# Four hybrid layers on one core: shared weight preparation, a merged second layer and a shorter buffer ring

## The chip, the cores and the metric

The kernel runs on one core of one Trainium2 chip, as a single launch. The metric is the device time in microseconds (us) of that launch. A profile of one execution gives the span from the first to the last instruction and, for each engine, what it did and what it waited for. The engines are PE (matrix products, with weight loads counted apart), DVE (vector), ACT (activations), POOL (a second vector engine) and SP, which here only issues transfers between DRAM and on-chip memory (SBUF). Products land in PSUM, in banks of 128 x 512 f32.

## The reference

The input is x of shape (4, 96, 64, 64). Four layers follow each other, and each adds its result to the stream. Batches never mix.

```python
# layer 0: layer norm, in_proj to xi and z, depthwise 3x3 conv, silu, selective scan, gate, MLP
xs = rows, columns, and both reversed           # 4 directions, 192 channels, 16 states
hst = hst * dA + dBx;  y_t = einsum('bkdn,bkn->bkd', hst, C_t)     # over 4096 steps
t = t + (layernorm(y_sum) * silu(z)) @ out_proj;  t = t + mlp(layernorm(t))
# layer 1: group norm, then
xc, z = in_proj(x);  u = silu(conv3x3(xc))
h = dA_l * h + dBu_l                            # 2 directions, 96 channels, 1 state
y = layernorm(y_forward + y_backward);  y = y * silu(z);  x = x + out_proj(y)
# layer 2: layer norm, relu(bn(x @ w1)), FFT over the 4096 tokens, complex relu, inverse FFT,
#          @ w2, bn; then layer norm and an MLP with e5m2 operands and f16 results ("ffn")
# layer 3: layer norm, linear attention (no softmax), then the same kind of ffn
```

## The kernel before, in words

**Two streams of work.** The *foreground* is the selective scan of layer 0: 64 steps (4 batches, 4 directions, 4 chunks of 1024 tokens), 24 units each, 1536 units in all. For a unit, `sources` has POOL multiply u and B into a tile `w`; `decays` has ACT form exp(dt A) into `h` in PSUM; `recurs` has DVE run the scan and then multiply by C into `w` (for every twelfth unit POOL does this product, in `side`); `gathers` has PE sum over states into `py`; `collects` adds that into `Y`. `preludes` makes dt, B and C for a step. The `w` tiles are a ring of `WB` = 7: POOL can write a tile again only when PE has read it. After each last-direction chunk, `Y` is stored to `y_d`; for batch 3, chunk 0 it stays in SBUF.

The *background* is everything else, in `others`: `front(b)` (norm, projection and conv of layer 0) for all batches, then `rest(b)` for batch after batch: `tail` (gate and MLP of layer 0, `gate(c)` for four chunks of 1024 and `group(g)` for eight groups of 512 tokens), `l1`, `l2_front`, `l2_middle`, `back`. `tail(b)` waits for the stores of `y_d`.

**The order** on every engine is fixed when the program is made. `Work` holds threads (generators). Each asks for an engine with `yield on(...)`, possibly with events, PSUM banks and a time. `Work.choose` takes the thread whose next piece could start first by estimated durations; ties go to the lower rank. What is then issued stands in order on that engine's queue, and an instruction that has to wait holds up everything behind it. `par(jobs, n, wide)` runs a list of jobs with n threads. While the foreground runs, the background has three PSUM banks (`bm`). When it has ended, five more (`be`) are opened and `mode["wide"]` is set: more threads, and elementwise work of the background goes to DVE instead of POOL (`spare`).

**Weights.** Each `rest(b)` loads its weights and prepares some: `tail` computes an MLP bias and centres `m1` (products with `cent` and a copy), `l1_weights2` multiplies two factors into `dtc`, `l2f_weights` folds a batch norm into `w1` (from a load `bn`, broadcast to 97 rows), `back_weights` folds another into `w2` and makes `wqt`, `wkv` and `vb`. For the last batch all but the tail's are made by `early`, right after the foreground.

**Layer 1 in the foreground's time** has stages with a barrier between: `inproj` (8 groups into the padded image `xp`), `conv` (9 matmuls per group and a silu into `u`), then 16 pieces: 8 forward, whose results stay in SBUF as `yf`, and 8 backward, which also finish the layer: centring, variance, the z projection into PSUM with its silu, the gate (`scalar_tensor_tensor(a, a, ..., pz)`), output projection, store to `t_d`. `l2_front` then loads `t_d` again for a layer norm into `xa` (`ln`), with a barrier, and computes the first FFT stage (`dft`). In wide mode conv already runs beside the pieces, and the pieces do the layer norm.

Lines in the profile are those of helpers: L205 is `mm`, L209 `copy`, L220 `act`, L217 its table load, L232 any DVE or POOL operation, L253 and L257 loads and stores. So work is told apart by tile names: `w<-u,bb` is POOL's product, `h<-h,state,w` a scan, `x_d`, `t_d` the stores of `x1_d` and `t_d`, `a<-a,vec,bm` the gate with z, `sc`, `var`, `vb`, `m`, `bias` the weight preparation.

## Time and profile before

| what | us |
|---|---|
| median of 3 runs | 6828.23 (6811.11 to 6831.17) |
| profiled execution, its own time | 6820.0 |
| its span | 6818.2 |
| DVE busy | 5834.1 (86%) |
| POOL busy | 4989.7 (73%) |
| PE busy | 5155.3 (76%), weight loads 1600.5 |
| ACT busy | 4259.4 (62%) |
| last scan of the foreground starts | 6167.8 |
| mean granted PE clock | 0.844 of full |

Busy times are shares of the whole span[...]. In a row of a group, the numbers behind the bar are the busy time in us, the mean duration of one in ns, and the idle time of that engine just before those instructions with what ended it. The scan's DVE rows carry most of the span. Up to about 140 us there is a start-up; after 6173 only batch 3 is left.

### The profile page before, as it was taken

The numbers are of one execution on the slowest core, as the hardware profiler recorded it, in microseconds if no ns is written. First come the engines' busy times: TensorE is split into PE (matmuls) and PEld (weight loads), VectorE is DVE, ScalarE is ACT, GpSimd is POOL, SyncE is SP. The second block draws the span as 40 slices with busy tenths as digits, with TensorE's granted clock in tenths as the row PEclk, the third lists the DMA queues.
The fourth block names the chain that finished last, engine by engine and source line by source line (L and its number), as shares of the span: only waits on it lengthen the run. The fifth ranks groups of instructions, "written<-read, shape, count | busy, mean of one in ns | idle before, by whom it ended". The sixth has DMA issues, their size and how long they took to land. (4 is left out here: it accounts for less than half of the span.)

```text
span 6818.2 us, 54968 instructions
## 1 busy us (share of the span) xinstructions
PE 5155.3 (76%) x15312; PEld 1600.5 (23%) x15312; DVE 5834.1 (86%) x3961; ACT 4259.4 (62%) x6433; POOL 4989.7 (73%) x2322
## 2 busy tenths in 40 slices
PE   7878897566866878768857787767876687777788
PEld 2222221111211332212201232212211133212263
DVE  3999999999998999999989999999989899992613
ACT  3757565465656557767656566776665555775735
POOL 2788888888897778887898777888789777871000
PEclk8889999687878999779878998877887898878888
DMA  5565555555545685565554586556555477533351
GB/s 161 186 197 180 189 176 178 164 181 172 166 148 156 216 263 159 163 191 177 167 159 148 173 280 193 165 166 194 162 157 155 152 234 248 173 111 82 114 154 34
DMA packets 522211, 1166.82 MB, mean 171 GB/s; under 512 B 90416, under 2 KB 163628, under 8 KB 521904
## 3 DMA queue, kind: packets, MB, share of 16 engines
q1 hardware_dynamic: 521904, 1163.31, 55.3%
q8 instruction: 122, 2.00, 0.1%
q14 instruction: 185, 1.52, 0.1%
HBM read 928.74 MB, written 234.36 MB: 171 GB/s over the span
## 5 line engine op out<-in xcount | busy, mean ns | idle before, releaser
L232 POOL TENSOR_TENSOR w<-u,bb 128x1024 f32<-128x1024 f32 x1536 | 3608.9, 2370 | 829.3 <-PE py L205 742.7
L232 DVE TENSOR_TENSOR_SCAN h<-h,state,w 128x1024 f32<-128x1024 f32 x1056 | 2480.4, 2349 | 149.7 <-ACT h L220 112.6
L205 PE MATMUL py<-w,sel 128*32 128x512 f32 x6144 | 1895.6, 953 | 788.9 <-DVE w L232 542.1
L220 ACT ACTIVATE h<-dt,negA 128x1024 f32<-128x1024 f32 x1536 | 1725.6, 1124 | 439.1 <-DVE w L232 378.2
L232 DVE TENSOR_TENSOR w<-h,cc 128x1024 f32<-128x1024 f32 x1408 | 1722.0, 1223 | 101.5 <-DVE h L232 3.7
L232 DVE TENSOR_TENSOR_SCAN h<-h,w 128x1024 f32<-128x1024 f32 x352 | 805.2, 2288 | 83.3 <-ACT h L220 72.1
L209 ACT COPY state<-h 128x1 f32<-128x1 f32 x1056 | 166.4, 158 | 906.5 <-DVE w L232 902.3
L205 PEld LDWEIGHTS py<-w,sel 128*32 128x32 f32 x6144 | 195.5, 117 | 1977.9 <-DVE w L232 1103.4
L232 POOL TENSOR_TENSOR w<-w,cc 128x1024 f32<-128x1024 f32 x128 | 301.5, 2355 | 105.6 <-ACT state L209 90.8
L205 PE MATMUL bm<-xp,dg 128*128 128x512 f32 x792 | 365.2, 610 | 1.3 <-ACT xi L220 1.3
L205 PE MATMUL bm<-xi,xw 128*128 128x512 f32 x384 | 233.9, 758 | 132.0 <-DMA xi<-xi_d 123.5
L205 PE MATMUL bm<-xd,dtw 64*128 64x512 f32 x384 | 230.2, 689 | 20.7 <-ACT dtu L220 7.2
L232 POOL TENSOR_TENSOR dtu<-dtu 128x1536 f32<-128x1536 f32 x64 | 221.7, 3464 | 30.1 <-ACT dtu L220 18.4
L220 ACT ACTIVATE dtu<-bm 128x512 f32<-128x512 f32 x384 | 208.3, 596 | 48.5 <-PE bm L205 45.2
L232 DVE TENSOR_TENSOR_SCAN w<-h,state,w 128x1024 f32<-128x1024 f32 x96 | 224.8, 2341 | 13.8 <-POOL w L232 7.1
L232 POOL MEMSET y<- 1x4096 f32 x4 | 14.1, 3514 | 291.7 <-DMA g_d<-o 291.6
L232 POOL TENSOR_TENSOR dtu<-dtu,xi 128x1536 f32<-128x1536 f32 x64 | 221.9, 3467 | 0.2
L205 PE MATMUL bm<-x,cent 96*96 96x512 f32 x318 | 183.8, 676 | 48.6 <-POOL x L232 13.7
L205 PE MATMUL bm<-xp,l1dg 96*96 96x512 f32 x468 | 215.8, 607 | 1.2 <-ACT u L220 1.2
L205 PEld LDWEIGHTS bm<-xp,dg 128*128 128x128 f32 x792 | 146.8, 192 | 267.8 <-issue 257.0
L232 POOL TENSOR_TENSOR Y<-Y,yt 128x512 f32<-128x512 f32 x141 | 182.8, 1296 | 29.4 <-ACT yt L209 28.2
L220 ACT ACT_TABLE_LOAD x131 | 168.1, 1283 | 20.3 <-PE bm L205 14.7
(356 smaller groups left out, 6956.2 us busy)
## 6 DMA issues: line engine op xcount, KB each, us to landing
u<-dd SPq DMA_DIRECT2D x384, 512.0 KB
dt<-dd SPq DMA_DIRECT2D x384, 512.0 KB
bb<-bc SPq DMA_DIRECT2D x256, 512.0 KB
cc<-bc SPq DMA_DIRECT2D x256, 512.0 KB
dd<-dtu SPq DMA_DIRECT2D x256, 384.0 KB
xi<-xi_d SPq DMA_DIRECT2D x256, 192.0 KB
f_d<-fo SPq DMA_DIRECT2D x64, 384.0 KB
a<-f_d SPq DMA_DIRECT2D x64, 384.0 KB
```

Of the source, the lines that this page charges most:

```text
L205: return nc.tensor.matmul(o, lhsT=lhsT, rhs=rhs, **kw)
L209: return nc.scalar.copy(o, i, **kw)
L220: return nc.scalar.activation(o, i, func, **kw)
L232: return f(o, *a, **kw)
```

## The change

It prepares the weights of the later layers once (`prepare`, in the background after `front(0)`), keeps them in one DRAM tile `prep` and loads them in packed pieces (`parcel`); constants that used to be loaded one by one are packed on the host. In layer 1, silu(z) is computed in `inproj`, stored to `z1_d` and loaded into a piece's own SBUF tile; forward results go to `y1_d` and come back; conv and pieces run together in both modes; backward pieces also do layer 2's norm. `xp` and `xa` share one tile, `big`. `dft` has three threads instead of two, the two f16 layers four instead of three, and `xq` lies inside `buf`. `WB` goes from 7 to 6. The diff, cut:

```diff
+    def fetch(self, load):
+
+        t = self.me
+        was = t.end, t.start, t.last
+        load()
+        t.start, t.last = was[1:]
...
+    prep = dram.tile([128, PREP], F32, name="prep_d")
+    y1_d = [dram.tile([C, L], F32, name=f"y1_d{b}") for b in range(B)]
+    z1_d = [dram.tile([C, L], F32, name=f"z1_d{b}") for b in range(B)]
...
-    def given(key, weights, wp, temp):
+    def given(key, weights, wp):
...
-        st, (wb,) = pools(bg(temp))
-        got = yield from weights(wp, wb)
-        st.close()
+        return (yield from weights(wp))
...
+    def parcel(wp, name, src, cols, sizes):
+
+        n = sum(w for _, w in sizes)
+        t = wp.tile([128, n], F32, name=name)
+        get(t, src[:, cols : cols + n])
+        got, c = [], 0
+        for rows, w in sizes:
+            got.append(t[0:rows, c : c + w])
+            c += w
         return got
...
     def tail(b, stat):
...
-        get(m1, I["mlp1T"])
-        get(wo, I["wo"])
-        get(m2, I["mlp2T"])
-        (pb,) = yield on("pe", banks=1)
-        for f in range(3):
-            mm(pb[:, f : f + 1], lhsT=m1[:, f * 128 : f * 128 + 128], rhs=V("b2", C), start=True, stop=True)
-        bias = wp.tile([128, 3], F32, name="bias")
-        yield on("dve")
-        ve.tensor_add(bias, pb[:, 0:3], V("mb1", n=3))
-        ve.tensor_scalar(m1, m1, V("g2", C), None, ALU.mult)
-        drop(pb)
-        yield from centred(m1, m1, 384)
+        wo, m2 = parcel(wp, "rt", I["r_tail"], 0, [(128, 6 * C), (128, 3 * C)])
+        m1, bias = parcel(wp, "pt", prep, 0, [(C, 384), (128, 3)])
+        wo = wo.rearrange("p (h j c) -> p h j c", h=2, j=3)
+        m2 = m2.rearrange("p (f c) -> p f c", f=3)
...
-    def l1_weights(wp, wb):
...
+    def l1_weights(wp):
...
-        get(gavg, I["c_gavg"])
-        get(w_in, I["l1_inT"])
-        get(dg, I["l1_dg"])
-        return gavg, w_in, dg
...
-    def l1_weights2(wp, wb):
...
-        yield on("pool")
-        po_.memset(dtc, 0.0)
...
-        (pw,) = yield on("pe", banks=1)
-        for k in range(2):
-            mm(pw[0:C, k * C : (k + 1) * C], lhsT=xr[:, k], rhs=dr[:, k], start=True, stop=True)
-        yield on("act")
-        copy(dtc[0:C, :, 0:C], pw[0:C, 0 : 2 * C].rearrange("p (k c) -> p k c", k=2))
-        drop(pw)
-        return w_out, dtc
...
-    def l1(b, stat, pp):
+        gavg, w_in, w_out = parcel(wp, "rl1", I["r_l1"], 0, [(C, C), (C, DI), (C, C)])
+        (dtc,) = parcel(wp, "pl1", prep, 387, [(C + 1, 2 * (C + 4))])
+        return gavg, w_in, w_out, dtc.rearrange("p (k c) -> p k c", k=2)
...
+    def l1(b, stat, pp, big):
         wide = mode["wide"]
-        stu, (pu,) = pools(bg("l1u"))
-        u = pu.tile([C + 1, L], F32, name="u")
-        st, (wp,) = pools(bg("l1c"))
-        xp = wp.tile([C, 66, 66], F32, name="xp")
-        gavg, w_in, dg = yield from given("l1", l1_weights, (pp, wp), "l1b")
+        u = pp.tile([C + 1, L], F32, name="u")
+        xp = big[0:C, 0 : 66 * 66].rearrange("p (h w) -> p h w", w=66)
+        xa = big[:, 0:L]
+        gavg, w_in, w_out, dtc = yield from given("l1", l1_weights, pp)
         mv = pp.tile([C, 2], F32, name="mv")
         gm = pp.tile([C, 4], F32, name="gm")
         bias = pp.tile([C, 2], F32, name="l1bias")
+        st, (wp, wk) = pools(bg("l1c"), bg("l1w"))
+        dg = wp.tile([C, 9, C], F32, name="dg")
...
+            po_.memset(big[C : C + 1], 1.0)
             po_.memset(u[C : C + 1], 1.0)
...
-        stx, (wk,) = pools(bg("l1cw"))
+        yield on("sp")
+        get(dg, I["l1_dg"])
 
         def inproj(g):
             def job(t):
-                x = wt(wk, C, "x", t)
+                x, z = wt(wk, C, "a", t), wt(wk, C, "dt", t)
+                s = slice(g * HC, (g + 1) * HC)
                 yield on("sp")
-                get(x, x1_d[b][:, g * HC : (g + 1) * HC])
+                get(x, x1_d[b][:, s])
...
+                post("l1x", b, g)
+                (pz,) = yield on("pe", banks=1)
+                mm(pz[0:C], lhsT=w_in[:, C : 2 * C], rhs=x, start=True, stop=True)
+                yield on("act", took=0.7, table=AF.Silu)
+                act(z, pz[0:C], AF.Silu, bias=bias[:, 1:2])
+                drop(pz)
+                yield on("sp")
+                put(z1_d[b][:, s], z)
 
...
-        yield from par([inproj(g) for g in range(NG)], 4, 8)
-        stx.close()
...
                 s = slice(q * HC, (q + 1) * HC)
+                near = ("l1x", b, min(q + 1, NG - 1))
                 if wide and t == 0:
+                    yield on("dve", near)
                     yield from taps(u[0:C, s], xp, 8 * q, V("l1cw", C, n=9))
-                    yield on("act", table=AF.Silu)
...
-                    return
-                (pc,) = yield on("pe", banks=1)
...
+                    pc = u[0:C, s]
+                else:
+                    (bank,) = yield on("pe", near, banks=1)
+                    pc = bank[0:C]
...
+                act(u[0:C, s], pc, AF.Silu, bias=V("l1cb", C))
+                if not (wide and t == 0):
+                    drop(bank)
                 post("l1u", b, q)
...
-        convs = par([conv(q) for q in range(NG)], 2)
-        if wide:
-            wk_.add(convs)
-        else:
-            yield from convs
-            st.close()
-
-        st2, (wp, wk) = pools(bg("l1s"), bg("l1sw"))
-        yf = wp.tile([C, L], F32, name="yf")
-        w_out, dtc = yield from given("l1s", l1_weights2, wp, "l1sb")
-        if wide:
-            xa = ahead["l2f"][4]
+        yield from par([inproj(g) for g in range(NG)], 3, 8)
+        convs = wk_.add(par([conv(q) for q in range(NG)], 2))
...
+                e2, name = spare()
                 yield on(name)
+                e2.tensor_mul(dt, a, cc[0:C])
                 if k == 0:
-                    e2.tensor_mul(yf[:, s], a, cc[0:C])
-                    post("l1y", b, g)
+                    yield on("sp")
+                    put(y1_d[b][:, s], dt)
+                    post("l1y", b, g, stored=True)
                     return
-                e2.tensor_mul(dt, a, cc[0:C])
-                x = bb
-                yield on("sp")
+                x, yf = bb, cc[0:C]
+                yield on("sp", ("l1y", b, g))
+                get(yf, y1_d[b][:, s])
                 get(x, x1_d[b][:, s])
-                pc, pv = yield on("pe", ("l1y", b, g), banks=2)
+                pc, pv = yield on("pe", banks=2)
                 mm(pc[0:C], lhsT=cent, rhs=dt, start=True, stop=False)
-                mm(pc[0:C], lhsT=cent, rhs=yf[:, s], start=False, stop=False)
+                mm(pc[0:C], lhsT=cent, rhs=yf, start=False, stop=False)
...
                 mm(pv[0:C], lhsT=avg, rhs=a, start=True, stop=True)
+                wk_.fetch(lambda: get(yf, z1_d[b][:, s]))
                 yield on("act", took=1.4, table=LN_EXP)
                 rstd(a, pv[0:C])
                 drop(pv)
                 yield on("dve")
                 ve.scalar_tensor_tensor(a, pc[0:C], V("l1og", C), a, ALU.mult, ALU.mult)
                 drop(pc)
-                (pz,) = yield on("pe", banks=1)
-                mm(pz[0:C], lhsT=w_in[:, C : 2 * C], rhs=x, start=True, stop=True)
-                yield on("act", table=AF.Silu)
-                act(pz[0:C], pz[0:C], AF.Silu, bias=bias[:, 1:2])
                 yield on("dve")
-                ve.scalar_tensor_tensor(a, a, V("l1ob", C), pz[0:C], ALU.add, ALU.mult)
-                drop(pz)
+                ve.scalar_tensor_tensor(a, a, V("l1ob", C), yf, ALU.add, ALU.mult)
                 (po,) = yield on("pe", banks=1)
...
-                if wide:
-                    pv = yield from norm(x, a)
-                    yield on("dve")
-                    ve.tensor_mul(xa[0:C, s], x, pv[0:C])
-                    drop(pv)
...
-        yield from par([piece(n) for n in range(2 * NG)], 3, 5)
...
-        stu.close()
-
-    def l2f_weights(wp, wb):
...
-        yield on("pool")
-        po_.memset(imp, 0.0)
-        po_.memset(xa[C : C + 1], 1.0)
-        yield on("sp")
-        get(bn, I["bn1"].partition_broadcast(C + 1))
...
-        yield on("act", table=LN_EXP)
-        rstd(sc, bn[:, 3, :])
-        yield on("dve")
-        ve.tensor_mul(sc, sc, bn[:, 0, :])
-        ve.tensor_mul(w1[0:C], w1[0:C], sc[0:C])
-        ve.tensor_mul(bn[:, 2, :], bn[:, 2, :], sc)
-        ve.tensor_sub(w1[C : C + 1], bn[C : C + 1, 1, :], bn[C : C + 1, 2, :])
-        yield from centred(w1[0:C], w1[0:C], DI)
-        return w1, rij, imp, mf1, xa
...
-    def l2_front(b):
...
-        st2, (wk2,) = pools(bg("l2fn"))
...
-        def ln(g):
...
-                yield on("sp")
-                get(x, t_d[b][:, s])
-                pv = yield from norm(x, rs)
+                pv = yield from norm(x, a)
                 yield on("dve")
                 ve.tensor_mul(xa[0:C, s], x, pv[0:C])
                 drop(pv)
...
-        if not mode["wide"]:
-            yield from par([ln(NG - 1 - i) for i in range(NG)], 3)
...
+        yield from par([piece(n) for n in range(2 * NG)], 3, 5)
+        st.close()
...
+    def l2f_weights(wp):
+        yield on("sp")
+        mf1, rij, imp = parcel(wp, "rl2", I["r_l2f"], 0, [(128, 128), (128, DI), (128, DI)])
+        (w1,) = parcel(wp, "pl2", prep, 587, [(C + 1, DI)])
+        return w1, rij.unsqueeze(1), imp, mf1
...
+    def l2_front(b, big):
+        xa = big[:, 0:L]
+        st, (wp, wk) = pools(bg("l2f"), bg("l2fw"))
+        w1, rij, imp, mf1 = yield from given("l2f", l2f_weights, wp)
...
-        yield from par([dft(q) for q in range(8)], 2, 4)
+        yield from par([dft(q) for q in range(8)], 3, 4)
...
-        xq = wt(wk, C, "xq", t, dt=E5M2)
+        xq = buf.bitcast(E5M2)[0:C, 4 * HC : 5 * HC]
...
-    def back_weights(wp, wb):
...
+    def back_weights(wp):
         yield on("sp")
-        get(var[:, 0, :], I["bn2"][3].partition_broadcast(C))
...
-        yield on("act", table=LN_EXP)
-        rstd(var, var)
-        rstd(vb[:, 0:1], V("bn2", C, 3))
...
+        mi2, wff, mask = parcel(wp, "rbk", I["r_back"], 0, [(128, 64), (C, C), (C, C)])
+        w2, wqt, wkv, vb = parcel(wp, "pbk", prep, 779, [(C, 2 * C), (C, C + 1), (C + 1, 2 * C), (C, 2)])
+        return w2.rearrange("p (h c) -> p h c", h=2), vb, mi2, wqt, wkv, wff, mask
...
-        yield from par([first(g) for g in range(NG)], 3, 5)
+        yield from par([first(g) for g in range(NG)], 4, 5)
...
-        yield from par([second(g) for g in range(NG)], 3, 5)
+        yield from par([second(g) for g in range(NG)], 4, 5)
...
+    def prepare():
+
+        st, (wp,) = pools(bg("prep"))
+        o = wp.tile([128, PREP], F32, name="prep")
+        m1, tbias = o[0:C, 0:384], o[:, 384:387]
...
+        yield on("pool")
+        po_.memset(o, 0.0)
+        yield on("sp")
+        get(m1, I["mlp1T"])
+        get(bn, I["bn1"].partition_broadcast(C + 1))
...
+        get(wq, I["l3_wq"])
+        (pb,) = yield on("pe", banks=1)
+        for f in range(3):
+            mm(pb[:, f : f + 1], lhsT=m1[:, f * 128 : f * 128 + 128], rhs=V("b2", C), start=True, stop=True)
+        yield on("dve")
+        ve.tensor_add(tbias, pb[:, 0:3], V("mb1", n=3))
+        ve.tensor_scalar(m1, m1, V("g2", C), None, ALU.mult)
+        drop(pb)
+        yield from centred(m1, m1, 384)
...
+        wk_.me.end += 15.0
+        yield on("act", took=1.5, table=LN_EXP)
+        rstd(sc, bn[:, 3, :])
+        rstd(var, var)
+        rstd(vb[:, 0:1], V("bn2", C, 3))
+        yield on("dve")
+        ve.tensor_mul(sc, sc, bn[:, 0, :])
...
+        yield on("sp")
+        put(prep, o)
+        sync()
...
-        yield from l1(b, stat, pp)
+        stb, (pb,) = pools(bg("big"))
+        big = pb.tile([C + 1, 66 * 66], F32, name="big")
+        stl, (pl,) = pools(bg("l1p"))
+        yield from l1(b, stat, pl, big)
+        stl.close()
+        yield from l2_front(b, big)
+        stb.close()
...
-        yield from l2_front(b)
...
-    WB, DB, RB, SIDE = 7, 3, 5, 12
+    WB, DB, RB, SIDE = 6, 3, 5, 12
...
+        yield from prepare()
```

## The prediction

> **What bounds it now.** I read first the busy time by stretches. The first row is the selective scan of layer 0 with all background work behind it, the second the rest of batch 3's tail, the third the later layers of batch 3. Columns: length, busy time of PE, weight loads, DVE, ACT and POOL with instruction counts, granted clock, DMA share, GB/s.
>
> ```profile
> 170.00:6155.00 5985.00, 4492.61 (x13228) 1278.35 (x13226) 5532.10 (x3497) 3841.26 (x5744) 4915.75 (x2262) 0.84 0.58 180
> ...
> 6173.00:6315.00 142.00, 116.03 (x254) 44.37 (x250) 44.03 (x48) 73.69 (x107) 13.18 (x11) 0.92 0.26 69
> 6315.00:6818.00 503.00, 409.35 (x1476) 225.36 (x1476) 191.92 (x333) 274.48 (x474) 5.87 (x2) 0.81 0.35 102
> ```
>
> For 5985 us DVE is 92% busy and nothing else is near it. After that DVE is mostly idle and chains of dependent steps set the pace. Second view, the costliest groups:
>
> ```profile
> L232 POOL TENSOR_TENSOR w<-u,bb 128x1024 f32<-128x1024 f32 x1536 | 3608.9, 2370 | 829.3 <-PE py L205 742.7
> L232 DVE TENSOR_TENSOR_SCAN h<-h,state,w 128x1024 f32<-128x1024 f32 x1056 | 2480.4, 2349 | 149.7 <-ACT h L220 112.6
> ...
> L232 DVE TENSOR_TENSOR w<-h,cc 128x1024 f32<-128x1024 f32 x1408 | 1722.0, 1223 | 101.5 <-DVE h L232 3.7
> ```
>
> All scans (2480.4+805.2+224.8+73.0) and products (1722.0) are 5305 us of DVE, none of it touched by the change. So the scan can end earlier only if DVE's other work or its idle time shrinks. Third view, the timeline where the scan ends:
>
> ```profile
> 6149.36 5.35 SPq L257 DMA_DIRECT2D out<-x  x2
> ...
> 6154.79 0.38 SPq L253 DMA_DIRECT2D m<-in_mlp1T  x1
> ...
> 6160.21 0.16 DVE L232 TENSOR_TENSOR bias<-bm,vec 128x3 f32<-128x3 f32 x1 [20.21 <-PE bm L205]
> ...
> 6167.80 2.35 DVE L232 TENSOR_TENSOR_SCAN w<-h,state,w 128x1024 f32<-128x1024 f32 x1 [7.11 <-POOL w L232]
> ```
>
> Batch 2's last output leaves at 6154 and only then does batch 3's tail begin (its first load, 6155), although three quarters of its input were stored at 5878, 5972 and 6057 (the y_d stores). The background is the late one: a background that runs faster hides batch 3's tail under the scan. Fourth view, batch 1's stages of layer 1: conv, forward scan, backward scan, layer 2 norm.
>
> ```profile
> 3295.00:3390.00 95.00, 90.15 (x274) 27.39 (x272) 89.93 (x53) 68.18 (x92) 74.81 (x32) 1.00 0.50 151
> 3390.00:3530.00 140.00, 73.81 (x171) 13.04 (x170) 125.48 (x83) 86.12 (x124) 136.11 (x74) 0.70 0.51 155
> 3530.00:3761.00 231.00, 155.80 (x350) 29.43 (x350) 206.69 (x143) 138.73 (x208) 202.53 (x105) 0.85 0.47 145
> 3761.00:3850.00 89.00, 61.05 (x191) 16.12 (x192) 76.00 (x59) 45.57 (x64) 66.93 (x28) 0.85 0.51 160
> ```
>
> The conv fills PE (90 of 95), the forward scan fills POOL (136 of 140); the norm stage fills nothing.
>
> **Background speed.** Conv and forward scan together: the scan's own PE share is gathers 1895.6 plus projections 233.9+230.2, over 5985, 0.39, so background PE is 90-37=53 in the conv and 74-55=19 in the forward scan, 72 us. A joint stage of 150 us leaves 150x0.61=91. POOL still needs its 140. So about 85 of 95 us go. The norm stage (89) goes; its five steps per piece move into the backward scan, whose 23 us per piece are some 25 steps with three threads: +25. The z projection moves to the input projection (35 us): +15 there, about -10 in the backward scan. A third dft thread: -15 of 104 at PE 91 of 104. Four threads in both f16 layers: -30 of 427, not a quarter, since there are three PSUM banks and ACT is at 177 of 220. Weight preparation: -13. Together about -190 us of a batch's 1340 after its tail.
>
> Each tail also waits for the scan. Batch 0 needed 91 us from the last y store (1585) to the last x1 store (1676). Batch 1's tail can end at 3110+91=3201, batch 2's at 4622+91=4713; batch 2 then ends at 4713+(6154-4871)-190=5806, before y(3,3) at 5878. With only 50 us saved per batch it is about 5963, still in time for most. So all of batch 3's tail but chunk 0 moves under the scan.
>
> **The sum**, as a shift of the profiled span of 6818.2 (its run took 6820.0; the median of the runs is 6828.2, 0.12% more).
>
> 1. *Weight preparation taken out of three batches.* DVE rows between 170 and 6140:
>
> ```profile
> L232 DVE SCALAR_TENSOR_TENSOR a<-a,vec,bm 96x512 f32<-96x512 f32 x24 | 17.4, 730 | 2.5 <-ACT bm L220 2.4
> ...
> L232 DVE TENSOR_TENSOR vb<-vb,vec 96x1 f32<-96x1 f32 x6 | 11.6, 1939 | 0.1
> L232 DVE TENSOR_TENSOR w<-w,var 96x192 f32<-96x192 f32 x3 | 7.0, 2328 | 0.3
> ...
> L232 DVE SCALAR_TENSOR_TENSOR hs<-imp,hs 128x192 f32<-128x192 f32 x3 | 5.1, 1706 | 0.0
> ...
> L232 DVE TENSOR_TENSOR sc<-sc,bn 97x192 f32<-97x192 f32 x3 | 1.1, 359 | 22.6 <-ACT state L209 19.2 <-ACT sc L220 3.4
> ...
> L232 DVE TENSOR_TENSOR bias<-bm,vec 128x3 f32<-128x3 f32 x3 | 0.5, 157 | 7.0 <-PE bm L205 7.0
> ```
>
> Before layer 2, ACT stood 11 us for the load of bn (at 3778), the decays behind it were late, and DVE idled 22.6 in all. With idle time: tail 0.5+7.0+6.0 (m<-m,vec), layer 2 22.6+1.1+3.2, back 7.0+11.6+4.1 (var)+0.5, **-63.6**.
>
> 2. *prepare(), once*, behind front(0): 11 such DVE instructions at about 1.6 us, 18, plus a wait like bias (2.3) and one more: **+22** (3 if short and unstalled, 36 if all last 2.4 and a load is late). Its 15 us delay in the plan stands for the bn load. The background that follows has slack: fronts ended at 1119, tail 0 first waited for y at 1306.
>
> 3. *End of the scan.* DVE idled 27 us around bias and the last scan, because PE and ACT stood 7 to 9 us for m before the last gathers. The preparation is gone: **-10** (0 to -20).
>
> 4. *Batch 3's tail now under the scan*, three chunks: two 1.75 us products, and two groups of 0.67+0.73+0.69, 7.7 each, 23, with a third more in waits: **+31**. The additions of two SBUF tiles go to POOL there.
>
> 5. *z from SBUF.* The row a<-a,vec,bm reads a and a PSUM bank; now it reads two SBUF tiles, and loses its PSUM bank. Here a rule speaks against the change: the Trainium skill's "SBUF — State Buffer", section "Who interferes with whom", says that a DVE instruction with two SBUF inputs shares a read interface with GpSimd, and whichever starts second waits for the whole of the other. Rows that read two SBUF tiles agree; after the scan, with POOL idle, the same ones are short:
>
> ```profile
> L232 DVE TENSOR_TENSOR w<-w,var 96x192 f32<-96x192 f32 x1 | 0.4, 355 | 0.0
> ...
> L232 DVE SCALAR_TENSOR_TENSOR hs<-imp,hs 128x192 f32<-128x192 f32 x1 | 0.3, 350 | 0.0
> ```
>
> By the rule, half of a 2.37 us POOL product, POOL busy 0.82: 0.97 each, 24 times, 23. By the nearest row, hs<-imp,hs, 1.71-0.35=1.36 each: 33. I take **+30** (0 to 47, the last at w<-w,var's 1.97).
>
> 6. *The w ring from 7 to 6, and the packed stage.* POOL runs one unit (2.35+1.22=3.57 us) less ahead. Pairing each POOL product with its scan in the timeline, w is done 12.6 us ahead at the median and under 4 us in eight places, most in forward scans: 0 to 8x3.57=29. SP gets 32 transfers more per batch (y1 and z1, stored and fetched, 192 KB each), less 8 reloads of t_d and 18 weight loads: +6 at about 0.4 us. But a store holds SP until POOL's or ACT's result is there, with the scan's u, dt, bb and cc loads behind it; the piece then waits for y1 to land. POOL waited 36 us for u<-dd before; some us more. **+15** (0 to 105, see the third rival).
>
> 7. *After the scan*: 142 us from the scan's end to the last x1 store become the chain of one chunk: gather, copy and sum 4.6 (6172.6 to 6177.2), then from the gate's first addition at 6255.0 to its second group's store at 6295.3, 40: 45. **-97** (-60 to -105).
>
> 8. *Layer 1 of batch 3*: ten table loads of 1.28 and eight 0.65 us silu leave the backward chain, eight matmuls, silus and one load enter the input projection, and y1 makes a trip through DRAM: **-3** (-13 to +8).
>
> Nothing is charged for parcels, the xq alias, the shared tile, or dropped POOL memsets (0.27 each; its 3.5 us row fill stays): POOL waits 743 us for PE as it is. Sum: -63.6+22-10+31+30+15-97-3 = **-75.6**: span 6743, median 6753.
>
> **Rivals.** (a) *The background hardly gains*: three PSUM banks already limit it, and two threads of conv take two of them. Against it: the norm stage fills no engine. Then half of batch 3's tail stays behind the scan, +50: 6803. (b) *All bounds kind*: no stretch of the z rows, a free ring, a cheap preparation, -10 more in layer 1: -30-15-10-10: 6688. (c) *Slower*: conv and forward scan in one stage fill PE and POOL together, with a shorter ring. POOL needs 2.98 us per unit for the scan (2.37, and 0.20, 0.29, 0.12 of w<-w,cc, dtu and Y) and some 51 us for 8 pieces. In 150 us the scan would run at 2.98/0.66=4.5 us per unit, against 4.1 in the forward scan before, 15 us per batch. It decides from 32 us per batch: (75.6+20)/3. Against it, w ran dry only in two of three forward scans, for 12 units at most. At 35: 6858.
>
> **How the numbers follow.** Likeliest 0.56, its own range 6715 to 6795; (a) 0.13; (b) 0.16; (c) 0.15. A change under 0.3% (20 us) can't be told from none here. Faster: 0.56+0.16, 0.07 of (a) and 0.02 of (c), 0.81; same: 0.06 and 0.03, 0.09; slower: 0.10. The range 6685 to 6830 leaves out half of (b) and two thirds of (c), 0.18.
>
> **What would show it.** Right: batch 2's last output before 5960; tail 3's stores of x1 before the scan's end except two; DVE rows sc, var, vb once each; a<-a,vec,cc near 2 us; span after the scan near 550. Wrong: the scan's end later than 6230 with DVE waiting for POOL's w, a joint stage over 200 us, or batch 3's tail still behind the scan.

## The result and the profile after

The changed kernel takes 6717.65 us (median of 4 runs, 6707.31 to 6725.84); the kernel before takes 6820.91 us beside it (4 runs, 6811.11 to 6831.17). The ratio is 0.985, 95% interval 0.982 to 0.987. The prediction was 6753, range 6685 to 6830. The profiled execution has a span of 6724.1 us and took 6725.84.

First the busy time of the changed kernel by the same three stretches (scan of layer 0; from its end to the last store of x1; the later layers of batch 3). Columns as before: length, busy time of PE, weight loads, DVE, ACT and POOL, granted clock, DMA share, GB/s.

```profile
170.00:6171.00 6001.00, 4512.15 (x13395) 1298.36 (x13396) 5554.00 (x3496) 3883.87 (x5792) 4952.50 (x2274) 0.84 0.59 184
6171.00:6226.00 55.00, 36.60 (x77) 12.97 (x75) 14.84 (x18) 18.22 (x24) 10.08 (x8) 0.84 0.20 57
6226.00:6724.00 498.00, 393.14 (x1456) 216.17 (x1456) 197.72 (x339) 255.47 (x460) 4.77 (x2) 0.82 0.40 116
```

The reader is to see that the first stretch did not become shorter. The middle one fell from 142 us to 55, the last from 503 to 498. The scan's own work is what it was, in the costliest groups:

```profile
L239 POOL TENSOR_TENSOR w<-u,bb 128x1024 f32<-128x1024 f32 x1536 | 3617.0, 2376 | 849.3 <-PE py L212 741.7
L239 DVE TENSOR_TENSOR_SCAN h<-h,state,w 128x1024 f32<-128x1024 f32 x1056 | 2480.2, 2349 | 173.5 <-ACT h L227 112.0
...
L239 DVE TENSOR_TENSOR w<-h,cc 128x1024 f32<-128x1024 f32 x1408 | 1722.2, 1223 | 107.7 <-DVE h L239 2.7
```

The timeline on the DMA queue of SyncE where batch 2 ends and batch 3's tail begins, and then where that tail ends (start, length, what is issued):

```profile
5944.93 0.32 SPq L264 DMA_DIRECT2D out<-x  x1
5945.34 0.38 SPq L260 DMA_DIRECT2D rt<-in_r_tail  x1
...
6171.96 2.88 SPq L264 DMA_DIRECT2D x_d<-x  x2
...
6221.51 2.89 SPq L264 DMA_DIRECT2D x_d<-x  x2
6224.96 4.37 SPq L260 DMA_DIRECT2D a<-x_d  x8
```

Batch 2's last output leaves at 5945, not 6154, so most of the tail runs under the scan. Of the eight stores of x1 (tensor x_d) four are issued before the scan's end at 6171 (6065 to 6118), two 1 and 3.5 us behind it, and the last two, those of the last chunk, at 6221.5 and 6224.1. The prediction had named all but two before the scan's end as a sign of being right; it was missed by these few us. And VectorE at the scan's end, where it used to idle for 27 us:

```profile
6165.04 2.35 DVE L239 TENSOR_TENSOR_SCAN h<-h,state,w 128x1024 f32<-128x1024 f32 x1
6167.49 1.23 DVE L239 TENSOR_TENSOR w<-h,cc 128x1024 f32<-128x1024 f32 x1
6168.64 2.34 DVE L239 TENSOR_TENSOR_SCAN w<-h,state,w 128x1024 f32<-128x1024 f32 x1
```

The last scan starts at 6168.64; before it was 6167.80. So the whole gain lies behind the scan: from its end to the end of the span 553 us instead of 648.

VectorE's rows of the background while layer 0 is scanned, the changed kernel:

```profile
L239 DVE SCALAR_TENSOR_TENSOR a<-a,vec,cc 96x512 f32<-96x512 f32 x24 | 43.2, 1799 | 0.0
...
L239 DVE TENSOR_TENSOR prep<-prep,sc 96x192 f32<-96x192 f32 x1 | 3.5, 3451 | 0.0
...
L239 DVE TENSOR_TENSOR sc<-sc,bn 97x192 f32<-97x192 f32 x1 | 1.4, 1360 | 0.0
L239 DVE TENSOR_TENSOR var<-var,gam 96x96 f32<-96x96 f32 x1 | 1.3, 1267 | 0.0
L239 DVE TENSOR_TENSOR gm<-mv,gm 96x1 f32<-96x1 f32 x3 | 0.5, 156 | 0.1
L239 DVE TENSOR_TENSOR gm<-gm 96x1 f32<-96x1 f32 x3 | 0.5, 156 | 0.1
L239 DVE TENSOR_TENSOR gm<-gm,mv 96x1 f32<-96x1 f32 x3 | 0.5, 156 | 0.1
```

The weight rows are there once instead of three times, and the 22.6 us of idle time before sc is gone. The gate's second product (a<-a,vec,cc), which now reads two SBUF tiles, takes 1.80 us instead of 0.73. The last three rows, steps of layer 1's group norm whose code did not change, were long before:

```profile
L232 DVE TENSOR_TENSOR gm<-gm 96x1 f32<-96x1 f32 x3 | 6.8, 2262 | 0.1
L232 DVE TENSOR_TENSOR gm<-mv,gm 96x1 f32<-96x1 f32 x3 | 5.5, 1844 | 0.1
L232 DVE TENSOR_TENSOR gm<-gm,mv 96x1 f32<-96x1 f32 x3 | 3.7, 1218 | 0.1
```

They fell by 16.0 - 1.5 = 14.5 us in all, which stood in no step of the sum.

The background's pace, from the trace's DMA issues, in us summed over batches 0 to 2. *Joint*: from the first load of layer 1's input projection to the first load of its backward scan. *Backward*: from there to layer 2's first spectrum store (f_d), so with the layer 2 norm. *dft*: to the first load of f_d. *First*, *second*: the two f16 layers, to the first load of gt and to the last output. The lower rows are experiments told below; they stand here so that each can be held against the others.

| kernel | joint | backward | dft | first | second | sum | batch 2 ends | last scan | last x1 store |
|---|---|---|---|---|---|---|---|---|---|
| before | 853 | 883 | 301 | 477 | 1385 | 3899 | 6154 | 6168 | 6314 |
| after | 842 | 764 | 229 | 417 | 1338 | 3590 | 5945 | 6169 | 6224 |
| e8 conv first | 945 | 774 | 232 | 440 | 1359 | 3750 | 6035 | 6179 | 6241 |
| e7 conv first, 3 threads | 1006 | 800 | 246 | 437 | 1409 | 3898 | 6152 | 6162 | 6298 |
| e3 gate in PSUM | 836 | 775 | 253 | 406 | 1318 | 3587 | 5926 | 6136 | 6190 |
| e9 e3 and conv first | 995 | 765 | 249 | 419 | 1335 | 3763 | 6064 | 6089 | 6231 |
| e10 e3 and 3 threads | 829 | 772 | 254 | 410 | 1360 | 3625 | 5946 | 6144 | 6199 |
| e11 less GpSimd | 748 | 795 | 232 | 420 | 1367 | 3562 | 5950 | 6168 | 6223 |
| e12 less TensorE | 754 | 859 | 244 | 410 | 1332 | 3599 | 5964 | 6179 | 6238 |

A batch's background became 103 us shorter ((3899 - 3590)/3), not 190. Joining the convolution with the forward scan, for which 85 of the 190 were counted, is in a stage that hardly moved. Its view by busy time, batch 1 of the changed kernel, joint and backward stage:

```profile
3253.00:3534.00 281.00, 193.58 (x522) 51.55 (x522) 250.52 (x160) 184.38 (x259) 251.11 (x125) 0.79 0.56 170
3534.00:3791.00 257.00, 193.80 (x504) 42.87 (x503) 250.06 (x176) 146.20 (x233) 216.00 (x102) 0.88 0.52 160
```

GpSimd (last of the five busy times) is busy for 251 of 281 us in the joint stage.

### The profile page after: what moved, and what is told of

Read it like the earlier page. It is cut to its first block, busy times and chain, and to the rows that moved or that the text cites. A ratio compares the mean times of both kernels' runs of the same rounds, so it can differ in the third digit from the quotient of the medians.

```text
span 6724.1 us, 54939 instructions
## 1 busy us (share of the span) xinstructions
PE 5070.8 (75%) x15240; PEld 1576.7 (23%) x15240; DVE 5827.8 (87%) x3933; ACT 4222.9 (63%) x6376; POOL 5010.5 (75%) x2319
## 5 line engine op out<-in xcount | busy, mean ns | idle before, releaser
L212 PE MATMUL py<-w,sel 128*32 128x512 f32 x6144 | 1823.9, 971 | 710.1 <-DVE w L239 524.7
L212 PE MATMUL bm<-big,dg 96*96 96x512 f32 x450 | 214.8, 624 | 5.1 <-ACT u L227 3.5
L212 PE MATMUL bm<-x,cent 96*96 96x512 f32 x272 | 158.1, 680 | 53.1 <-DMA x<-in_x 18.5
L239 DVE TENSOR_TENSOR h<-bm,rs 96x512 fp8e5<-96x512 f32 x54 | 36.7, 679 | 162.2 <-ACT rs L227 155.2
```

The lines of the kernel that those rows point to most:

```text
L212: return nc.tensor.matmul(o, lhsT=lhsT, rhs=rhs, **kw)
L239: return f(o, *a, **kw)
```

## The experiments

**The tail's place.** Batch 3's tail is kept back until the last scan is issued, so that all of it comes behind:

```diff
 # tail(b), ahead of its jobs
+        if b == B - 1:
+            yield on(None, ("scans",))
 # the scan, behind each unit
+            if i == NU - 1:
+                post("scans")
```

> The changed kernel, but batch 3's gates and groups of the tail wait until the foreground's last scan has been issued; all else stays. My theory: hiding that tail under the scan is the main gain. Held back, the stretch from the last scan to the last x1 store grows from 55 us to about 140 (142 before), and the scan itself ends some 30 us earlier, since 23 us of DVE products and their waits leave it: about +55, 6770 us. Rival, the gain comes from the weight preparation and the shorter layer 1, and the tail would have been short anyway: within 15 us of 6718.

Measured: 6783.13 us, ratio 0.995 (0.993 to 0.997) to before, 65 us more than the changed kernel. Its timeline at the last scan:

```profile
6128.96 1.23 DVE L239 TENSOR_TENSOR w<-h,cc 128x1024 f32<-128x1024 f32 x1
6130.10 2.34 DVE L239 TENSOR_TENSOR_SCAN w<-h,state,w 128x1024 f32<-128x1024 f32 x1
```

The last scan starts 38.5 us earlier (6168.64 - 6130.10), which is what three chunks of tail cost under the scan, and the last x1 store comes at 6289, 159 us behind it instead of 55. The place of the tail is the larger part of the gain; without it a third of the change is left (0.995 against 0.985). That third is the scan itself: without the tail in it, it starts its last unit 38 us earlier than in the kernel before (6130.10 against 6167.80).

**The ring.** The kernel before with the w ring of the change:

```diff
-    WB, DB, RB, SIDE = 7, 3, 5, 12
+    WB, DB, RB, SIDE = 6, 3, 5, 12
```

> The kernel before with a ring of 6 w tiles instead of 7, nothing else. My theory: the median lead of POOL's product over its scan falls from 12.6 to about 9 us, and the time grows by the few places where POOL then comes too late, 5 to 29 us: 6826 to 6850 us, near 6836. Rival, the ring is what makes the changed kernel's first chunk of batch 0 finish 41 us later (1347 against 1306): then the same lateness, 40 us or more by the first y store and more later on: 6860 us or above.

Measured: 6832.27 us, ratio 1.003 (1.002 to 1.004): 15 us by the medians, 21 by the ratio, and the last scan 6 us later. The first y store comes 6 us later too (1312 against 1306), not 40, so the ring is not what makes that store late in the changed kernel. GpSimd's lead over the scan, pairing each product with its scan in the timeline, falls from 12.6 to 8.8 us at the median, about one unit of 3.57. The other direction, a ring of 7 in the changed kernel, was not run.

**The gate.** The changed kernel with the gate's first product left in its PSUM bank, so that neither product reads two SBUF tiles:

```diff
-                ve.scalar_tensor_tensor(a, pc[0:C], V("l1og", C), a, ALU.mult, ALU.mult)
-                drop(pc)
+                ve.scalar_tensor_tensor(pc[0:C], pc[0:C], V("l1og", C), a, ALU.mult, ALU.mult)
                 yield on("dve")
-                ve.scalar_tensor_tensor(a, a, V("l1ob", C), yf, ALU.add, ALU.mult)
+                ve.scalar_tensor_tensor(a, pc[0:C], V("l1ob", C), yf, ALU.add, ALU.mult)
+                drop(pc)
```

> The changed kernel, but the first of the two gate products of a layer 1 piece writes into its PSUM bank instead of SBUF, so that the second reads one PSUM and one SBUF tile. The bank is held one DVE step longer. My theory: the second product took 1.80 us instead of 0.73 because it read two SBUF tiles beside POOL; it falls back to about 0.75, and as DVE sets the scan's pace, 24 x 1.07 = 25 us are gained: 6693 us. Rival, such a wait is hidden by the slack that DVE has before each scan (decays late): the row gets short but the time stays within 8 us of 6718. Second rival, the PSUM bank held longer slows the background: batch 2 ends later than 5945.

Measured: 6695.7 us, ratio 0.982 (0.980 to 0.984), 22 us less than the changed kernel; the last scan starts 32 us earlier. The row's stretch, 24 x (1.80 - 0.73) = 26 us, is paid by the scan about one for one.

**The preparation.** First prepare() behind all fronts instead of behind the first:

```diff
         yield on(None, ("front", 0))
-        yield from prepare()
         for b in range(1, B):
             yield from front(b)
+        yield from prepare()
```

> The changed kernel, but the weights are prepared after the fronts of all batches instead of after the first, where the background waits for the first y anyway. My theory: the 41 us by which the first y store is late come in good part from prepare and the four fronts behind it, which start 80 us later and then run beside the first loads; moved, the first y store comes 15 to 30 us earlier and the time falls to about 6700. Rival, the lateness is the ring's, or the preparation costs the same 15 us of DVE wherever it stands: within 8 us of 6718.

Measured: 6694.68 us, ratio 0.982 (0.980 to 0.984). The time fits, the reason does not: y's first store is at 1338 us instead of 1347, 9 us earlier and not 15 to 30. The scan, held against the kernel before unit by unit, is 9.6 us late at unit 240 and 34.9 at unit 288, so prepare() costs 20 to 25 us where it now stands (the changed kernel, whose preparation is long done there, slips 5 us over the same units), as it cost the changed kernel 22 by unit 48. It costs the same in either place; the 23 us came later, in no one place that the trace shows. VectorE's timeline in that stretch:

```profile
1166.55 0.15 DVE L239 TENSOR_TENSOR prep<-bm,vec 128x3 f32<-128x3 f32 x1
1166.61 11.90 DVE L239 TENSOR_SCALAR prep<-prep,vec 96x384 f32<-96x384 f32 x1
1178.44 2.34 DVE L239 TENSOR_TENSOR_SCAN h<-h,state,w 128x1024 f32<-128x1024 f32 x1
```

Half of the 25 us is one instruction; in the changed kernel the same one takes 0.65 us (at 164.31). More of it below.

Then ahead of the first scan, where VectorE has little to do, alone and with the gate's edit:

```diff
-        yield from prepare()
...
-        first = wk_.add(setup()), wk_.add(front(0))
-        wk_.run(lambda: first[0].done and ("inproj", 0) in wk_.events)
+        first = wk_.add(setup()), wk_.add(front(0)), wk_.add(prepare())
+        wk_.run(lambda: first[0].done and first[2].done and ("inproj", 0) in wk_.events)
```

> The changed kernel with prepare() moved alone, ahead of the first scan, beside setup() and front(0); the gate is left as changed. Theory: the scan loses 22 to 24 us to prepare() wherever prepare() stands behind it, and nothing when it stands where VectorE idles: 6718 - 22, about 6695 us, with the scan at unit 240 within 10 us of the kernel before. Rival: the start-up is itself a chain of loads, sums and matmuls, and prepare()'s steps lengthen it: the first scan starts 15 to 25 us later and the time is within 8 us of 6718.

> The changed kernel with two edits: prepare() runs as a third job beside setup() and front(0) ahead of the first scan, where VectorE has nothing to do for 54 us, and the gate keeps its first product in PSUM, so that neither of its two products reads two SBUF tiles. Theory: the two costs are separate, 22 to 24 us of scan for prepare() (the scan fell behind by that much where prepare() stood, in two places) and 21 us for the gate (measured alone). Both go: 6718 - 22 - 21, about 6675 us, ratio near 0.979, and the last scan near 6168 - 44 = 6124. Rival: the background's two costs fill the same idle time of VectorE, so that taking both away gives no more than one of them: about 6695. Second rival: prepare() ahead of the scan delays the scan's start by what it saves: then also about 6695.

Measured: alone 6703.69 us, ratio 0.984 (0.981 to 0.987); with the gate 6689.18 us, 0.982 (0.980 to 0.985). The first scan starts at 163 us instead of 142: the start-up is a chain itself, and prepare() makes it 21 us longer. So the rivals come nearer: prepare() costs 20 to 25 us in each of three places, and the second edit adds nothing that can be told from the gate alone (0.982 both). Not all is explained. Alone, the move gave 14 us by the medians, between theory and rival and within the intervals of the ratios (0.984 and 0.985), and in the profiled execution the last scan starts 23 us earlier than in the changed kernel, though the first starts 21 later. The three versions with 0.982 (gate in PSUM, preparation late, preparation in the start-up with the gate) beat both kernels and can't be ranked among themselves.

**The background's speed.** In the changed kernel, forward scan behind the whole convolution again, alone and together with three threads in the f16 layers:

```diff
-        convs = wk_.add(par([conv(q) for q in range(NG)], 2))
+        convs = par([conv(q) for q in range(NG)], 2)
+        if wide:
+            wk_.add(convs)
+        else:
+            yield from convs
 # e7 only
-        yield from par([first(g) for g in range(NG)], 4, 5)
+        yield from par([first(g) for g in range(NG)], 3, 5)
-        yield from par([second(g) for g in range(NG)], 4, 5)
+        yield from par([second(g) for g in range(NG)], 3, 5)
```

> The changed kernel with one part undone: the forward scan of layer 1 waits for the whole convolution again while layer 0's scan is running; four threads stay. Theory: GpSimd, 88% busy through the joint stage, set its length, so that joining saved only about 35 us per batch, not the 85 predicted; batch 2 ends near 5980 (35 us later than 5945), and since batch 3's tail still fits under the scan the time stays within 10 us of 6718. Rival: the joint stage costs the scan time, since it puts more GpSimd work beside it with a shorter ring: then undoing it makes the kernel faster by 10 to 30 us.

> The changed kernel with two parts of the change undone, both of which only make the background faster: the forward scan of layer 1 waits for the whole convolution again, and both f16 layers go back from four threads to three. Theory: batch 2 ends at 5945 in the changed kernel and batch 3's tail needs about 91 us per chunk of work behind its inputs, the last of which is stored at 6089; so there is slack of about 100 us. The convolution beside the scan gained about 35 us per batch and the fourth thread about 30; without both, batch 2 ends near 6010 to 6030, three quarters of batch 3's tail still fits under the scan, and the time is within 15 us of 6718. Rival: the background speed is what the whole gain rests on, as the prediction has it; the loss adds up over three batches, batch 2 ends behind 6080, a part of batch 3's tail comes out from under the scan and the time is 6740 to 6770.

Measured: conv first 6755.97 us, ratio 0.992 (0.989 to 0.994), 38 us more than the changed kernel (21 in the profiled executions); both 6797.14 us, 0.998 (0.997 to 0.998). Both theories of mine failed. In the table, the joint stage is longer by 34 us per batch in e8 ((945 - 842)/3), as expected. But batch 2 ends 90 us later, not 35: its layer 1 starts 28 us later, its joint stage is 42 us longer, and its later stages lose 20. In e7 the background needs 3898 us, as much as in the kernel before (3899): batch 2 ends at 6152, and all of batch 3's tail is behind the scan, 136 us from last scan to last x1 store. The loss of batch 2's end, 207 us, was twice as large as the slack of some 100 us that I had read from the trace.

Part of e8's loss was another thing. Its row of the gate, in the same window:

```profile
L239 DVE SCALAR_TENSOR_TENSOR a<-a,vec,cc 96x512 f32<-96x512 f32 x24 | 71.3, 2972 | 0.0
```

The same instruction as in the changed kernel, 2.97 us instead of 1.80, 28 us more in all (in e7 2.94, 27 us more). So both edits were run once more on top of the gate in PSUM, where this can't happen:

> The changed kernel with the gate's first product in PSUM, and with the forward scan of layer 1 waiting for the whole convolution again. To be held against the same kernel without the second edit (6696 us, ratio 0.982, last scan at 6136). Where the convolution came first without the first edit, the products that read two SBUF tiles had become longer, 2.97 us each instead of 1.80, 28 us in all, some of them 9 to 11 us beside four to six GpSimd products in a row. Theory: these made most of that run's loss; with the product in PSUM they are 0.73 us each, the last scan stays within 8 us of 6136, batch 2 ends some 80 us later than 5926, at about 6006, still ahead of the last of the tail's inputs, and the time is 6696 to 6712 us. Rival: the order of convolution and scan costs the time by itself, as 6756 against 6718 says, and the time is about 6734.

> The changed kernel with the gate's first product in PSUM, and with three threads in the two f16 layers instead of four. To be held against the same kernel without the second edit (6696 us). Theory: the fourth thread saves about 10 us per batch in the first f16 layer and 20 in the second (three PSUM banks serve four threads), so that batch 2 ends 30 to 50 us later than 5926; the tail's last inputs are stored behind 6057, so nothing comes out from under the scan and the time is within 10 us of 6696. Rival: the fourth thread is worth 41 us by itself, the difference of 6797 and 6756 when the convolution came first: about 6737.

Measured: conv first 6745.44 us, ratio 0.990 (0.988 to 0.992), 50 us more than e3 (39 in the profiled executions); three threads 6704.35 us, 0.984 (0.982 to 0.985), 9 us more. For the convolution the rival was right: undoing the join costs the time by itself. How, is in one row of the busy time of e9, from its last scan's end to its last x1 stores:

```profile
6092.00:6236.00 144.00, 115.88 (x251) 43.47 (x249) 42.48 (x45) 74.06 (x101) 10.68 (x8) 0.90 0.27 71
```

From the last scan to the last x1 store it is 142 us, about as long as the 146 of the kernel before. Its last scan starts at 6089, 47 us earlier than in e3; but batch 2 ends at 6064, and the tail has only begun. A faster scan ran away from a slower background. Why the scan is faster is known in part: about 18 of the 47 us come while e3 has its tail in the scan and e9 has not, but 29 are there already when e3's tail begins, 12 of them before the first joint stage. Over the first 1440 units VectorE idles 26 us less in e9; what took that idle time away was not followed. In e8 the scan was held up, to 6179, so that less of the tail stood behind it (61 us from last scan to last x1 store).

Three threads cost 14 us per batch in the second f16 layer, about nothing in the first, and batch 2 ends 20 us later, inside the slack: theory right, its 30 to 50 us too many. The 148 us by which e7's background is slower than e8's is therefore not the fourth thread alone: 61 of it are in the joint stage, which that edit doesn't touch. The program's order is written from estimates for all the instructions at once, so each edit also moves others; which moves these were was not followed.

**What sets the joint stage.** GpSimd at 251 of 281 us was the suspect. Two variants of the changed kernel, in each of which part of layer 1 is left out while layer 0 is scanned. The first leaves out two of the forward scan's GpSimd products per piece, the second six of the nine matmuls of each piece of the convolution and the two points inside it at which other threads get their turn:

```diff
 # e11, in piece()
-                e2.tensor_mul(a, dt, u[0:C, s])
-                yield on(name)
-                e2.tensor_mul(a, a, bb)
+                if k or wide:
+                    e2.tensor_mul(a, dt, u[0:C, s])
+                    yield on(name)
+                    e2.tensor_mul(a, a, bb)
 # e12, in conv()
-                    for k in range(9):
+                    taps_ = range(9) if wide else (0, 4, 8)
+                    for k in taps_:
...
-                        if k in (2, 5):
+                        if wide and k in (2, 5):
```

> The changed kernel without two multiplications in each piece of layer 1's forward scan while layer 0's scan runs (dt times u and the product with bb), so the output is not the reference's: 16 instructions of 1.27 us on GpSimd per batch, 20 us. It is read by the length of the joint stage, from the input projection's first load to the backward scan's first load: 280, 281 and 281 us in the changed kernel, 842 in all, with GpSimd busy for 251 to 253 of each. Theory: GpSimd sets the length of this stage, so it loses about 20 us in each batch: 842 becomes 770 to 795. Rival: the stage is set by TensorE and its chain of steps: each stays within 6 us and the sum over 825.

> The changed kernel with three of the nine matmuls in each of the eight pieces of layer 1's convolution while layer 0's scan runs, so the output is not the reference's: 48 matmuls of about 0.6 us less per batch, 29 us of TensorE. It is read by the length of the joint stage, 280, 281 and 281 us in the changed kernel, 842 in all, with TensorE busy for 194 to 199 of each. Theory: GpSimd sets the length of this stage and TensorE does not: each stays within 8 us, and the sum is 820 to 845. Rival: TensorE, shared with the scan's gathers and projections at a granted clock of 0.75 to 0.79, sets it: the sum falls by 60 to 90, to 755 to 785.

Measured: 6725.7 us (ratio 0.987, 0.985 to 0.989) and 6743.41 us (0.989, 0.987 to 0.991). By the joint stage the theory had the direction for GpSimd (748, even below its 770 to 795) and fell for TensorE: 754, next to the rival's 755 to 785. The stage gives back whichever is taken, 31 us per batch for 20 us of GpSimd and 29 for 29 of TensorE. But the next stage differs, in the busy time of batch 1, joint and backward. e11:

```profile
3252.00:3502.00 250.00, 178.81 (x476) 47.87 (x478) 221.34 (x145) 170.54 (x242) 205.30 (x101) 0.77 0.54 165
...
3502.00:3764.00 262.00, 190.59 (x510) 44.09 (x510) 243.33 (x174) 146.23 (x229) 212.98 (x102) 0.85 0.54 163
```

e12:

```profile
3243.00:3480.00 237.00, 141.03 (x364) 32.65 (x360) 207.92 (x134) 160.06 (x232) 215.83 (x110) 0.71 0.56 170
...
3480.00:3782.00 302.00, 211.41 (x544) 49.21 (x544) 282.68 (x191) 157.87 (x247) 235.84 (x112) 0.79 0.51 152
```

With fewer matmuls the backward stage became longer by what the joint one saved: 754 + 859 = 1613 for both stages over three batches, against 842 + 764 = 1606 in the changed kernel. With less GpSimd work it is 748 + 795 = 1543, 63 us less for 60 us left out. That points to GpSimd over the two stages together, but it is a reading that was formed behind the result; what bounds the joint stage taken alone is not settled. In e11 GpSimd was busy for only 82% of it (205 of 250 us, against 251 of 281 in the changed kernel), so at that length it did not set the stage alone. Neither kernel is faster than the changed one: with batch 2's end at 5950 the tail already waits for the scan's own stores of y.

## Why the prediction was right, and where it was not

The time was within the range and the direction right: 35 us below the 6753. Of these, 19 are in the sum (span 6743 forecast, 6724 measured); the rest is that the median lies 6 us below the profiled span, where 10 above it had been taken. By the sum's steps:

- *The sum at the scan's end* was +24.6 (steps 1 to 6) and measured +0.8. Steps 2, 4, 5 and 6 were about as costed: the preparation +22 (20 to 25 in three places), the tail's three chunks +31 (38.5), the gate +30 (26 by its row, 32 by the last scan), the ring's part of step 6 6 us at the last scan and 15 by the medians, where +15 stood for ring and staging together.
- *Step 3, "DVE idled 27 us around bias and the last scan", costed at -10 (0 to -20)*, is the term that was mis-sized: no idle time is left in the rows at the scan's end, so it is about -27. I had taken away a part of the stall for the preparation, though the whole start of the tail leaves that place.
- *Step 1* left out the three gm rows, 14.5 us. Their code is unchanged; they read two small SBUF tiles. Before, seven of the nine ran beside GpSimd's products; now all nine run beside its memset of `big`, which reads no tile, and take 156 ns each. That was luck of their place (in e7 gm<-gm takes 0.9 us each again). With step 3's 17 these are 31 us too much cost, and the tail's chunks, 7 above their estimate, go the other way, which leaves the 24. The run with the tail held back agrees: without the tail the steps had -7 and the last scan started 38 us earlier, 31 more.
- *Step 6, the staging*: the late loads of the scan that it feared came, but not where the staging is. From the list of waits (total us, times, longest), before:

```profile
POOL w L232 <- DMA u<-dd: 48.2, 15, 11.2
ACT h L220 <- DMA dt<-dd: 25.9, 10, 12.3
```

and after:

```profile
ACT h L227 <- DMA dt<-dd: 87.6, 24, 13.9
POOL w L239 <- DMA u<-dd: 81.6, 25, 13.4
```

  The scan's loads come late more often, 95 us more for the two together. Of the 169 us after, 49 stand ahead of 260 us, beside prepare(), where the kernel before had 4, and 42 more before 1144, beside the fronts (14 before). In the stretches in which y1 and z1 are stored and fetched (1700 to 2300, 3200 to 3860 and 4700 to 5300) it is under 3 us in all. Little of it reached VectorE, whose idle time before scan work rose by 41 us (297 to 338, without the start-up), ring included. What the staging alone costs was not measured.
- *Steps 7 and 8* were right: 142 to 55 (45 forecast), 503 to 498 (500).
- *Background speed, "about -190 us of a batch's 1340"*, was wrong by nearly half: -103. (Its own terms add to -202.) The step that failed is "Conv and forward scan together: ... A joint stage of 150 us". From the input projection's end to the backward scan's first load it takes 224 us in batch 1 (3310 to 3534), past the 200 that I had named as a sign of being wrong. Undone, it costs 34 us per batch in its stage, not 85; and the z projection, in an input projection that now has three threads instead of four, took about 31 of that again (e8's joint stage 945 against 853), where 15 had been counted. In the step itself PE was checked against an average share and GpSimd against the 140 us of the old forward stage alone, and not against what it does for the scan in the rest of the time. That sum stands in rival (c), 2.98 us per unit for the scan and 51 us for the pieces, but there the scan was made to give way. With the scan at the pace that it had before, 3.93 us per unit (6026 us for 1535 units), the same figures leave GpSimd 24% of the time for the pieces, and their 51 us (53 by their rows in the changed kernel) take 211: an estimate made behind the result, near the 224. It can't be the whole account, since by it the 20 us left out in e11 would have given back some 80 and gave 31. The norm with the backward scan gained 40 us per batch where 74 had been counted (-89, +25, -10), dft 24 (15), f16 layers and their weights 36 (43).
- *"With only 50 us saved per batch it is about 5963, still in time for most"*: by the sum ahead of it, 4713 + (6154 - 4871) - 50, it is 5946. e8 is this case, (3899 - 3750)/3 = 50, and batch 2 ended at 6035. I had let each tail end 91 us after the last y store of the kernel before (1585, 3110, 4622); in e8 those stores come at 1613, 3137 and 4678, 27 to 56 us later, and its batch 2 saved less than the mean of the three. The time was right by luck in this: half the forecast gain was just enough, 5945 against tail inputs stored at 5888, 5989 and 6089.

Of the rivals, (a) was wrong in its consequence although its premise, a background that hardly gains from the convolution, was the true one. (b) didn't come: gate, preparation and ring cost what they were charged. (c) did not come either: with GpSimd busy for 89% of the joint stage the scan kept its pace (GpSimd made 55 of its w products in the 224 us, 4.07 us each, as 67 in the 267 us from 3295 to 3562 before, 3.99; over all three joint stages it is 3.97 us per scan, 4.01 before), and the stage became longer than planned. Here the background gave way, not the scan.

## What to carry to other kernels

When background work has to be done before a foreground ends, cost the margin and not the saving: here two edits to the background were worth 80 us (some 27 of them the gate's row), since they brought batch 2's end ahead of the tail's inputs; 20 us more of background inside that margin (e10) cost 9 us, which the intervals do not separate from nothing; and where the scan ran 47 us ahead of a slower background the tail came out behind it. Before two stages are joined, add up what every engine does in both, the foreground's share at its present pace included; in 150 us the scan at that pace takes 114 us of GpSimd (2.98 of every 3.93), and the 51 of the pieces do not fit beside it. A VectorE product moved from PSUM to SBUF should be costed as a range that depends on where GpSimd happens to be (1.80 to 2.97 us here, against 0.73), and put back into PSUM where a bank is free.

## What was not expected of the hardware

The gate's second product, once both of its tiles were in SBUF, took 1.80 us on average in the changed kernel, 1.07 above 0.73, with single ones from 0.72 to 3.42. In e8 single ones took far longer. VectorE there:

```profile
2089.48 1.22 DVE L239 TENSOR_TENSOR w<-h,cc 128x1024 f32<-128x1024 f32 x1
2090.61 8.91 DVE L239 SCALAR_TENSOR_TENSOR a<-a,vec,cc 96x512 f32<-96x512 f32 x1
2099.45 2.34 DVE L239 TENSOR_TENSOR_SCAN h<-h,state,w 128x1024 f32<-128x1024 f32 x1
```

and GpSimd beside it, one row for five products in a row:

```profile
2087.30 11.67 POOL L239 TENSOR_TENSOR w<-u,bb 128x1024 f32<-128x1024 f32 x5
```

VectorE's product, at work since 2090.61, ended at 2099.52, 0.55 us behind the last of the five (2098.97), although three of the five began after it. It is so throughout these traces: all 39 of these products that took over 1 us, 19 in the changed kernel and 20 in e8, ended 0.54 to 0.61 us behind the end of some GpSimd instruction. Which one differs. In the changed kernel it was the first to end in 16 of 19. In e8 further ones went ahead in 10 of 20, and one product took 10.9 us. A gap in GpSimd's work is not needed. In the changed kernel:

```profile
2110.94 2.81 DVE L239 SCALAR_TENSOR_TENSOR a<-a,vec,cc 96x512 f32<-96x512 f32 x1
...
2110.79 7.46 POOL L239 TENSOR_TENSOR w<-u,bb 128x1024 f32<-128x1024 f32 x3
```

VectorE's product ended at 2113.75, behind the first of these three. 10 of the 19 came in so, between two GpSimd instructions that follow each other without idle time, and the GpSimd instruction behind them was then some 0.45 us longer (2.8 us for w<-u,bb, elsewhere mostly 2.35). So both engines can hold each other up; what decides who goes next no run here shows.

The prediction weighed a rule of the Trainium skill ("SBUF — State Buffer", "Who interferes with whom") by which a VectorE instruction with two SBUF inputs waits for one whole GpSimd instruction, and took half a product, 0.97 us, as the mean. The mean fits the changed kernel, 1.07; the wait for one instruction only does not hold in e8.

The 11.90 us tensor_scalar of e4 stands beside GpSimd work without a gap too (1164.59 to 1178.30, five instructions), ending 0.2 us behind it, though it has only one SBUF tile to read beside its column of scalars; the same section names tensor_scalar among the operations that can take both ports. In the changed kernel the same instruction took 0.65 us.

So the gate's product cost 1.80, 1.92 (e6) or 2.97 us on average by where the order of the program put it, and single ones up to fifteen times the 0.73 us that it took in every run with one of its tiles in PSUM.
